# The token search of a mixture-of-experts layer: tile table as weights, lane table moving, sums transposed

## The chip, the cores and the metric

The kernel runs on one core of one Trainium2 chip. The metric is the device time of one execution in microseconds (us). A core has five engines that run side by side and wait for each other by semaphores: TensorE (matrix products; PE in the profile, its weight loads PEld), VectorE (DVE), ScalarE (ACT), GpSimd (POOL) and SyncE (SP, which here starts DMA transfers and reads numbers out of memory). A product on TensorE has two operands in SBUF, the core's working memory of 128 partitions: the *weights* are loaded into the array first (LDWEIGHTS), and then the *moving* operand streams through it, column by column. The sums go to PSUM.

## The reference, cut to what matters

A layer of attention plus a mixture of eight experts over 4096 tokens of 128 numbers. Each token is sent to its two best experts.

```python
scores = x @ gate_w.T                       # x: 4096 tokens x 128, E = 8 experts
mult, idx = _route(scores)                  # the two best experts, with their factors
g = (one_hot(idx, E) * mult[..., None]).sum(axis=1)
h1 = einsum('th,efh->tef', x, w1)
h3 = einsum('th,efh->tef', x, w3)
inter = silu(h1) * h3 * g[:, :, None]
y = einsum('tef,ehf->th', inter, w2)
...
x = x + _L0_attn_ref(xn, ...) + _L0_ffn_ref(xn, ...)
```

## The kernel before

Tokens lie in 32 blocks of 128 (`TT`), one token to a partition, and are handled in two halves `u` (`NU`) of 16 blocks (`UT`). `route(u)` finds each token's two experts and, by counting, the place that the token takes among all tokens of that expert.

The experts' work is cut into 71 tiles of up to 128 tokens (`NSLOT`: 64, and 7 for the remainders). A tile belongs to one expert; within it a token has a *lane*, 0 to 127. So each of the two choices `c` (`TOP`) of a token has an address: a tile (`found_at[u][:, 0]`) and a lane (`found_at[u][:, 1]`).

The *search* turns this around: for every tile and lane it finds the token that belongs there. It does so with products. `in_lanes(u)` builds on VectorE a table `lane[u, c]` of 0 and 1, partition x 128 lanes x 16 blocks (f16, `qb`, `vb`, `oT` and `x2` buffers): 1 where the token has that lane. `slots()` builds a table `tile_{u}_{c}` (called `v`), partition x 71 tiles x 16 blocks: 1 where the token belongs to that tile (L441), multiplied by the token's number (L444). For each block `t` one product of the two sums over the 128 partitions, and 32 products add up in PSUM to `found[:, c]`, lanes by tiles: the number of the one token there, or zero. In all 64 products (2 choices x 2 halves x 16 blocks). In both tables the block is the innermost index, so `[:, :, t]` reads every 16th f16 number, a step of 32 bytes.

`tokens_of(found)` on VectorE makes of it the lists `token` (which row of `table` to gather), `row` (where the result is added) and `first_of`. Ahead of it, while VectorE waits for the products, `slots()` computes `past`, `own_f`, `own` and `fresh` (the expert of each tile, and whether its weights must be fetched anew, L453 to L458).

The order of the instructions is written by hand and is fixed on every engine. Around the search it is:

- on TensorE, 80 products of ones (`busy_late`, L1251) are issued ahead of the search; after it come the first projections of the attention (`pq`, `pqs`, L799), the transposes of `v` (`pvt`, L856), the transposes of gathered tokens (`pxs`, L537) and the experts' first products (L552);
- on VectorE, `tokens_of` is followed by `bias` (L669, L670) and the rotations of `k` and `q` (L813 to L848);
- POOL gathers the tokens of a tile by an indirect DMA (`fetch`, L501), with `token` as its list;
- SP reads `own` and `fresh` and fetches an expert's weights (`weights`, L527); the second and third fetch wait for a gather.

After this comes the long loop over the 71 tiles, in which the experts' products and the attention's work are woven together by a planner; it is not touched.

PSUM is divided into pools: `pa` with five buffers, `ph` with two and `py` with one. `found` lies in `py`, which the `pxs` transposes use afterwards. `busy_late` and later the experts' sums lie in `ph`. In SBUF the tables `tile_{u}_{c}` and `past` use the tag `gT`, with five buffers in turn.

Of the kernel before, what the change touches and what calls it, by code (L numbers as in the profile page):

```python
# [11 lines left out]
F32 = mybir.dt.float32  # L12
# [18 lines left out]
P = 128  # L31
# [16 lines left out]
TOP = 2  # L48
NSLOT = TOP * TT + E - 1
# [35 lines left out]
def attn_moe_kernel(ctx: ExitStack, tc: tile.TileContext, a: dict, out: bass.AP):  # L85
    nc = tc.nc

    const = ctx.enter_context(tc.tile_pool(name="const", bufs=1))
    sb = ctx.enter_context(tc.tile_pool(name="sb", bufs=2))
# [3 lines left out]
    ph = ctx.enter_context(tc.tile_pool(name="ph", bufs=2, space=bass.MemoryType.PSUM))  # L93
    py = ctx.enter_context(tc.tile_pool(name="py", bufs=1, space=bass.MemoryType.PSUM))

    def bc(ap, axis, n):
        shape = list(ap.shape)
        shape.insert(axis, n)
        return ap.unsqueeze(axis).to_broadcast(shape)
# [39 lines left out]
    ident = const.tile([P, P], F32, tag="ident", name="ident")  # L139
# [136 lines left out]
    def tmp(shape, tag, name, dt=F32):  # L276
        return sm.tile([P, *shape], dt, tag=f"r_{tag}", name=f"{tag}_{name}", bufs=NU)
# [114 lines left out]
    lane = {}  # L392
# [10 lines left out]
    def slots():  # L403

        count = tmp([E], "count", 0, I32)
        whole = tmp([E], "whole", 0)  # L410
        nc.vector.tensor_tensor(whole, counts[:, 0], counts[:, 1], ALU.add)
        yield
        nc.vector.tensor_scalar(count, whole, float(P - 1), None, ALU.add)
        yield
        nc.vector.tensor_scalar(count, count, 7, None, ALU.logical_shift_right)
        yield
        nc.vector.tensor_copy(whole, count)
        yield
        end = tmp([E], "end", 0)
        nc.vector.tensor_tensor_scan(end, ones[:, 0:E], whole, 0.0, ALU.mult, ALU.add)  # L420
        yield
        base = tmp([E], "base", 0)
        nc.vector.tensor_tensor(base, end, whole, ALU.subtract)
        yield
        for u in range(NU):
            big = sb.tile([P, TOP, UT, E], F32, tag="rope", name=f"base_{u}", bufs=3)
            nc.vector.tensor_tensor(
                big, hots[:, :, ts(u, UT), :], bc(bc(base, 1, UT), 1, TOP), ALU.mult
            )
            yield  # L430
            at = tmp([TOP, UT], "tile", u)
            nc.vector.tensor_reduce(at, big, AX.X, ALU.add)
            yield
            nc.vector.tensor_tensor(found_at[u][:, 0], found_at[u][:, 0], at, ALU.add)
            yield
        yield True
        found = py.tile([P, TOP, NSLOT], F32, tag="py", name="found")
        for c in range(TOP):
            for u in range(NU):
                v = sb.tile([P, NSLOT, UT], F16, tag="gT", name=f"tile_{u}_{c}", bufs=5)  # L440
                nc.vector.tensor_tensor(  # L441
                    v, ramp[:, 0:NSLOT], bc(found_at[u][:, 0, c], 1, NSLOT), ALU.is_equal
                )
                nc.vector.tensor_tensor(  # L444
                    v, v, bc(number_of[:, ts(u, UT)], 1, NSLOT), ALU.mult
                )
                for t in range(UT):
                    nc.tensor.matmul(  # L448
                        found[:, c], lhsT=lane[u, c][:, :, t], rhs=v[:, :, t],
                        start=(u == 0 and t == 0), stop=(u == NU - 1 and t == UT - 1),  # L450
                    )
        past = sb.tile([P, NSLOT, E], F32, tag="gT", name="past", bufs=5)
        nc.vector.tensor_tensor(past, bc(tile_start, 2, E), bc(end, 1, NSLOT), ALU.is_ge)  # L453
        own_f = tmp([NSLOT], "own_f", 0)
        nc.vector.tensor_reduce(own_f, past, AX.X, ALU.add)
        nc.vector.tensor_scalar(own, own_f, float(E - 1), None, ALU.min)
        nc.vector.tensor_tensor(
            fresh[:, NW_BUF:], own_f[:, NW_BUF:], own_f[:, : NSLOT - NW_BUF], ALU.not_equal  # L458
        )
        tokens_of(found)  # L460

    def tokens_of(found):

        sum_f = tmp([NSLOT], "sum_f", 0)
        nc.vector.tensor_copy(sum_f, found[:, 1])
        nc.vector.tensor_tensor(sum_f, found[:, 0], sum_f, ALU.add)
        nc.vector.scalar_tensor_tensor(token, sum_f, 0.0, sum_f, ALU.is_gt, ALU.subtract)
        nc.vector.tensor_scalar(token, token, NTOK - 1, None, ALU.bitwise_and)
        empty = tmp([NSLOT], "empty", 0)
        nc.vector.scalar_tensor_tensor(empty, sum_f, 0.0, spare, ALU.is_equal, ALU.mult)  # L470
        nc.vector.tensor_tensor(row, token, empty, ALU.add)
        nc.vector.tensor_scalar(first_of, found[:, 0], 0.0, None, ALU.not_equal)
# [710 lines left out]
    with tc.manual_schedule(  # L1183
# [4 lines left out]
        parts = [moments(u) for u in range(NU)]  # L1188
        turns = []
        folds, finding = fold(), slots()  # L1190
        act, dve, pool = nc.scalar, nc.vector, nc.gpsimd
        plan = Plan(
# [200 lines left out]
```

## Time and profile before

| what | us |
|---|---|
| median of three runs | 463.5 |
| the three runs | 462.41, 463.5, 468.3 |
| the profiled execution | 465.26 |
| its span, first to last instruction | 463.5 |
| TensorE, products busy | 419.1 (90%) |
| VectorE busy | 315.4 (68%) |
| ScalarE busy | 254.0 (55%) |
| POOL busy | 241.6 (52%) |

The span is what the profile shows; the execution's own time has 1.8 us more around it. All times "at" something are microseconds from the start of the span. The search's place in it:

| at (us) | what |
|---|---|
| 43.2 to 52.3 | `busy_late` on TensorE |
| 45.1 to 51.7 | the four `lane` tables on VectorE, with other work between |
| 51.7 to 57.5 | the four `tile` tables on VectorE, two instructions each |
| 53.2 to 62.1 | the 64 products of the search |
| 57.4 to 59.3 | `past`, `own_f`, `own`, `fresh` on VectorE |
| 62.1 to 63.7 | `tokens_of` on VectorE |
| 64.5 | the first gather on POOL |
| 69.4 | the first product of the first expert tile |

A line of a timeline reads: start, duration, engine, line and operation, what is written and read, shapes, count, and in brackets how long the engine was idle just before and what ended it. A product's recorded duration is the time from its start to its end, which overlaps the next ones; the time from one start to the next tells how fast they follow. The granted clock is the share of TensorE's full clock that it is given at the time.

### The profile page before, as it was taken

How to read it: one execution, taken by the hardware profiler on the slowest of the kernel's cores; microseconds unless marked ns; L12 is line 12 of the kernel's file. 1: busy time of each engine (PE TensorE's matmuls, PEld its weight loads, DVE VectorE, ACT ScalarE, POOL GpSimd, SP SyncE). 2: the span in 40 equal slices, each digit the busy share in tenths (PEclk: the TensorE clock that was granted, in tenths of full speed). 3: DMA queues.
4: the chain of work that ended last, by engine and by line, in shares of the span. 5: the costliest groups of instructions: out<-in, count | busy, mean ns of one | idle time of the engine just before them, and what ended most of it. 6: DMA issues, size and time to landing. Idle time of an engine off the chain costs nothing.

```text
span 463.5 us, 11704 instructions
## 1 busy us (share of the span) xinstructions
PE 419.1 (90%) x4547; PEld 358.1 (77%) x4547; DVE 315.4 (68%) x750; ACT 254.0 (55%) x716; POOL 241.6 (52%) x210
## 2 busy tenths in 40 slices
PE   9859998999997999999999999999999998999900
PEld 9427966898886899869789888797988897989800
DVE  5698977788788897686676876874868567434300
ACT  1466014888326969534956795339767823553300
POOL 0724237776457454476464466664454657532442
PEclk9986958999999999999999999999999999999975
DMA  8710755226412722352145522451365224516314
GB/s 249 259 47 2 141 125 166 30 25 150 99 19 35 197 39 31 86 144 30 26 96 150 58 26 36 114 127 24 78 148 75 35 37 96 132 18 114 75 17 51
DMA packets 43670, 39.51 MB, mean 85 GB/s; under 512 B 3056, under 2 KB 41968, under 8 KB 43616
## 3 DMA queue, kind: packets, MB, share of 16 engines
q1 hardware_dynamic: 26896, 27.29, 20.7%
q0 software_dynamic: 16720, 11.49, 19.9%
q8 instruction: 36, 0.59, 0.5%
q14 instruction: 18, 0.15, 0.1%
HBM read 60.16 MB, written 11.04 MB: 154 GB/s over the span
## 4 chain that ended last, share of the span: by engine, by line
PE 65%; DVE 13%; ACT 12%; DMA 5%; issue 3%; SPq 0%; POOLq 0%; POOL 0%; DVEq 0%
PE y L578 11%; PE p L552 11%; PE y L552 8%; ACT pr L920 5%; PE pf L1032 5%; PE po L950 5%; DMA out_dram<-sly,row 3%; PE pff L1043 3%; PE ppt L930 3%; PE ps L878 3%; PE found L448 2%; PE px L976 2%; DVE mx L895 2%; PE pgt L265 2%; PE pqs L799 2%
## 5 line engine op out<-in xcount | busy, mean ns | idle before, releaser
L597 POOL DMA_INDIRECT out_dram<-sly,row x71 | 112.3, 1582 | 140.3 <-ACT sly L588 74.6
L501 POOL DMA_INDIRECT slx<-table,token x71 | 71.1, 1001 | 34.8 <-issue 18.5
L562 DVE SCALAR_TENSOR_TENSOR th<-th,p 128x512 f32<-128x512 f32 x71 | 48.6, 684 | 50.2 <-ACT th L561 50.0
L552 PEld LDWEIGHTS p<-slxT,w 128*128 128x128 f32 x568 | 70.2, 192 | 15.4 <-issue 10.2
L578 PEld LDWEIGHTS y<-w,it 128*128 128x128 f32 x568 | 69.6, 191 | 15.7 <-issue 6.4
L578 PE MATMUL y<-w,it 128*128 128x128 f32 x568 | 77.8, 280 | 2.7 <-DVE it L567 2.7
L552 PE MATMUL p<-slxT,w 128*128 128x128 f32 x568 | 78.0, 280 | 1.9 <-issue 1.2
L561 ACT ACTIVATE th<-p 128x512 f32<-128x512 f32 x71 | 44.1, 622 | 57.6 <-PE p L552 49.5
L588 ACT ACTIVATE sly<-y,wt 128x128 f32<-128x128 f32 x71 | 28.0, 394 | 71.5 <-PE y L552 69.3
L567 DVE TENSOR_TENSOR it<-y,th 128x384 f32<-128x384 f32 x70 | 38.8, 554 | 37.9 <-ACT sly L588 37.8
L552 PE MATMUL y<-slxT,w 128*128 128x128 f32 x420 | 58.3, 275 | 0.0
L920 ACT ACTIVATE pr<-ps,mx 128x64 f32<-128x64 f32 (+1 forms) x256 | 54.5, 372 | 0.1
L552 PEld LDWEIGHTS y<-slxT,w 128*128 128x128 f32 x420 | 52.5, 192 | 0.0
L895 DVE TENSOR_REDUCE mx<-ps 128x8 f32<-128x512 f32 x64 | 41.5, 684 | 3.3 <-PE ps L878 2.7
L938 ACT COPY pT<-ppt 128x512 f32<-128x512 f32 (+1 forms) x64 | 35.4, 623 | 0.7
L930 PE MATMUL ppt<-ident,pr 128*128 128x128 f32 x240 | 33.3, 274 | 1.2 <-ACT pr L920 1.1
L1032 PE MATMUL pf<-hT,wf1g 128*128 128x512 f32 x64 | 32.4, 599 | 0.9 <-ACT gT L1036 0.7
L1043 PE MATMUL pff<-pack,gT 128*128 128x128 f32 x256 | 32.7, 275 | 0.0
L961 DVE RECIPROCAL rz<-po 128x256 f32<-128x256 f32 x16 | 28.1, 1756 | 4.2 <-PE po L950 4.0
L1043 PEld LDWEIGHTS pff<-pack,gT 128*128 128x128 f32 x256 | 30.6, 192 | 0.0
L930 PEld LDWEIGHTS ppt<-ident,pr 128*128 128x128 f32 x240 | 27.4, 141 | 3.2 <-ACT pr L920 2.1
L1036 ACT ACTIVATE gT<-pf,bf1g 128x512 f32<-128x512 f32 x32 | 21.8, 693 | 6.8 <-PE pf L1032 6.8
(178 smaller groups left out, 657.2 us busy)
## 6 DMA issues: line engine op xcount, KB each, us to landing
w<-in_wexp_dram SPq DMA_DIRECT2D x71, 704.0 KB
out_dram<-pack SPq DMA_DIRECT2D x1, 2112.0 KB
table<-xn SPq DMA_DIRECT2D x2, 1040.0 KB
x<-in_x_dram SPq DMA_DIRECT2D x8, 256.0 KB
out_dram<-x POOLq DMA_DIRECT2D x8, 256.0 KB
slx<-table,token POOLq DMA_INDIRECT x71, 2.7
out_dram<-sly,row POOLq DMA_INDIRECT x71, 3.3
pack<-in_pack_dram SPq DMA_DIRECT2D x1, 898.0 KB
```

The costliest lines, as they stand in the source:

```text
L501: i = nc.gpsimd.indirect_dma_start(out=self.group[g][:, c, :], out_offset=None, in_=table[:, :], in_offset=bass.IndirectOffsetOnAxis(ap=to ...
L552: nc.tensor.matmul(self.p[j, k][:, c, :], lhsT=self.w[j][:, ts(NFC * k + c, P)], rhs=self.xT[j], start=True, stop=True,)
L561: nc.scalar.activation(th, p, AF.Tanh, scale=0.5)
L562: nc.vector.scalar_tensor_tensor(th, th, 1.0, p, ALU.add, ALU.mult)
L567: nc.vector.tensor_tensor(self.it[j][:, 0:3], self.p.pop((j, 1))[:, 0:3], self.th.pop(j)[:, 0:3], ALU.mult)
L578: nc.tensor.matmul(p[:, 3], lhsT=it[:, c, :], rhs=w[:, 2 * F + c * D : 2 * F + (c + 1) * D], start=(c == 0), stop=(c == NFC - 1),)
L597: nc.gpsimd.indirect_dma_start(out=out[:, :], out_offset=bass.IndirectOffsetOnAxis(ap=row[:, j : j + 1], axis=0), in_=y, in_offset=None, c ...
L895: nc.vector.tensor_reduce(mx, v.rearrange("p s c g k -> p s g c k"), AX.XY, ALU.max, negate=True)
L920: nc.scalar.activation(to[:, s, c0:, g], v[:, s, c0:, g], AF.Exp, bias=mx[:, s, g : g + 1])
L930: nc.tensor.transpose(pp[:, ts(k, P)], v[:, k // 2, k % 2].rearrange("p g k -> p (g k)"), ident)
L1032: nc.tensor.matmul(pf, lhsT=wf1g[:, ts(c, P)], rhs=self.hT[b], start=True, stop=True)
L1043: nc.tensor.matmul(self.pf[b][:, ts(t, D)], lhsT=self.gT[b, c][:, ts(t, P)], rhs=wf2[:, c, :], start=(c == 0), stop=(c == NDF - 1),)
```

## The change

The two tables change places in the products: `tile_{u}_{c}` becomes the weights (71 columns instead of 128) and `lane[u, c]` the moving operand (128 columns instead of 71). The sums then lie with the tiles on the partitions and the lanes along the row, in a PSUM buffer `by_tile` of the pool `ph`. Since `tokens_of` needs lanes on the partitions, the sums are copied by VectorE into an SBUF buffer `lines` (tag `gT`) after `fresh`, and TensorE transposes the two halves of it into `found`, which stays in `py`. What is computed is the same.

```diff
@@ -434,7 +434,7 @@
         yield True
-        found = py.tile([P, TOP, NSLOT], F32, tag="py", name="found")
+        by_tile = ph.tile([NSLOT, TOP, P], F32, tag="ph", name="by_tile")
         for c in range(TOP):
             for u in range(NU):
                 v = sb.tile([P, NSLOT, UT], F16, tag="gT", name=f"tile_{u}_{c}", bufs=5)
...
                 for t in range(UT):
                     nc.tensor.matmul(
-                        found[:, c], lhsT=lane[u, c][:, :, t], rhs=v[:, :, t],
+                        by_tile[:, c], lhsT=v[:, :, t], rhs=lane[u, c][:, :, t],
                         start=(u == 0 and t == 0), stop=(u == NU - 1 and t == UT - 1),
                     )
         past = sb.tile([P, NSLOT, E], F32, tag="gT", name="past", bufs=5)
@@ -457,6 +457,11 @@
         nc.vector.tensor_tensor(
             fresh[:, NW_BUF:], own_f[:, NW_BUF:], own_f[:, : NSLOT - NW_BUF], ALU.not_equal
         )
+        lines = sb.tile([NSLOT, TOP, P], F32, tag="gT", name="lines", bufs=5)
+        nc.vector.tensor_copy(lines, by_tile)
+        found = py.tile([P, TOP, NSLOT], F32, tag="py", name="found")
+        for c in range(TOP):
+            nc.tensor.transpose(found[:, c], lines[:, c], ident[0:NSLOT, 0:NSLOT])
         tokens_of(found)
```

## Prediction

> **What bounds the kernel now.** I read the page first, then the timeline from 52 to 80 us, then the rows of line 448, and last the busy table by window of the clock.
>
> The page says who owns the end:
>
> ```profile
> PE 419.1 (90%) x4547; PEld 358.1 (77%) x4547; DVE 315.4 (68%) x750; ACT 254.0 (55%) x716; POOL 241.6 (52%) x210
> ...
> PE 65%; DVE 13%; ACT 12%; DMA 5%; issue 3%; SPq 0%; POOLq 0%; POOL 0%; DVEq 0%
> PE y L578 11%; PE p L552 11%; PE y L552 8%; ACT pr L920 5%; PE pf L1032 5%; PE po L950 5%; DMA out_dram<-sly,row 3%; PE pff L1043 3%; PE ppt L930 3%; PE ps L878 3%; PE found L448 2%; PE px L976 2%; DVE mx L895 2%; PE pgt L265 2%; PE pqs L799 2%
> ```
>
> TensorE carries 65% of the chain that ends last, and the search (`found`, L448) has 2% of it, some 9 us. Nothing runs beside the search that could fill in: the engines' orders are fixed, and the expert loop cannot start without the list of tokens. The timeline shows the handover:
>
> ```profile
> 55.98 0.74 DVE L441 TENSOR_TENSOR tile<-ramp,at 128x1136 f16<-128x1136 f16 x1
> 56.76 0.75 DVE L444 TENSOR_TENSOR tile<-tile,number_of 128x1136 f16<-128x1136 f16 x1
> ...
> 62.03 0.20 PEld L799 LDWEIGHTS pq<-nT,wallg 128*32 128x32 f32 x8 [0.22 <-issue]
> 62.04 1.08 PE L799 MATMUL pq<-nT,wallg 128*32 128x256 f32 x8
> 62.14 0.23 DVE L465 COPY sum_f<-found 128x71 f32<-128x71 f32 x1 [2.82 <-PE found L448]
> ...
> 63.87 0.20 PEld L799 LDWEIGHTS pqs<-nT,wallg 128*32 128x32 f32 x8 [1.63 <-DVE bias L670]
> ...
> 64.46 1.23 POOL L501 DMA_INDIRECT slx<-table,token  x1 [15.45 <-DVE bias L670]
> ```
>
> VectorE has the last one-hot table at 57.5 us and then idles 2.8 us for TensorE, so the 64 products are what ends last here. Behind them everything queues: VectorE's `sum_f` to `bias`, hence ScalarE's `kb`, POOL's first gather, TensorE's own `pqs`. Whatever the search gains or loses up to 62.14 us moves the rest as a block.
>
> What limits one product? The rows of line 448, the first load alone, and two other lines' rows:
>
> ```profile
> L448 PEld LDWEIGHTS <-lane x64: 142/147/157, 52.1 to 61.7; 128*128 128x128 f16 x64
> L448 PE MATMUL found<-tile,lane x64: 298/317/323, 53.2 to 61.8; 128*128 128x71 f16 x64
> ...
> 52.09 0.15 PEld L448 LDWEIGHTS <-lane 128*128 128x128 f16 x1
> ```
> ```profile
> L683 PEld LDWEIGHTS pbf<-pack,pack x8: 186/192/192, 72.0 to 72.8; 128*128 128x128 f32 x8
> L683 PE MATMUL pbf<-pack,pack x8: 250/250/271, 72.0 to 72.8; 128*128 128x1 f32 x8
> ```
> ```profile
> 54.70:56.00 1.30, 1.30 (x12) 1.00 1.23 178
> 56.00:57.80 1.80, 1.80 (x15) 0.50 1.29 200
> 57.80:61.95 4.15, 4.15 (x32) 0.50 0.94 142
> ```
>
> Starts from 53.2 to 61.8 us over 63 steps: 136 ns for a pair of load and product. The last fence (stretch, then PE busy with its count, then granted clock) shows that the clock falls from 1.00 to 0.50 at 56.0 us and the pace does not change with it. So the array's clock is not the limit; reading an operand is. Which one? The `pbf` rows show a pair that waits for its weights: the product moves one column, eight pairs start within 0.8 us (some 111 ns each), and a load recorded at 192 ns thus holds its path for about 111, 81 less. Line 448's load is recorded at 147, the lone first one too; less the same 81 it holds its path for some 66 ns, half of the 136. Its product is recorded at 317 where `busy_late`'s, of 128 f32 columns, has 275. I conclude that the moving operand sets the pace: 71 columns in 136 ns, 1.92 ns per column. Both tables are read with a step of 16 halves (32 bytes, `[:, :, t]`), which no other row here does. The Trainium skill (Advanced Engine Details and Errata, Memory Cachelines) gives a reason: reads pay when each element lies in a new 16-byte line.
>
> **Part 1: the operands change places.** The moving operand grows from 71 to 128 columns at the same step of 32 bytes. No row shows a moving table of 128 such columns, so I bound it. From below: it streams at the clock, and the pace falls to that or to the load's. From above: loads and products stop overlapping, 381 ns (worked out among the rivals). The row it is nearest to is line 448's own moving read, as step, type and memory are the same: 128 x 1.92 = 245 ns.
>
> Here a rule and the row part. The Trainium skill (TensorE: Matmul & The Clock Gate, Back-to-back issue gap) gives an isolated product N/1.2 ns at half clock: 59 for 71 columns, 107 for 128. By it the new pace would be 107, 64 x (107 - 136) = -1.9 us before the transposes. But the same rule predicts 59 for what the trace shows at 136, so I use the row: 63 x 245 = 15.5 us, plus the last product (0.34 us from its start at 61.80 to VectorE's at 62.14, plus 0.11 for its longer stream), 15.9 in all, against 62.14 - 53.23 = 8.9. That is **+7.0 us**.
>
> The weights shrink from 128 to 71 columns. A rule speaks against this too: the same page (Weight-path perf modes) says that a non-f32 weight of exactly 128 columns is loaded in four chunks of 32 at once; with 71 that ends. Line 448's 66 ns for 128 columns agree with chunks (32 x 1.92 = 61). Loading 71 one after another would be 136 ns by the row's rate, 59 by the page's P/1.2. Either is under 245 and is pulled ahead of the running product, as now: 0. Its cover is the longer stream; without it the price is rival 3. Only the first load loses its head start (it ran at 52.09, before the table; now it waits for the table): +0.1 us.
>
> VectorE's tables come every 1.45 us (0.74 + 0.75 less overlap), while 16 products would take 3.9: tables stay hidden. `past`, `own`, `fresh` end at 59.3 us and SP's first fetch of weights goes at 59.88, unchanged.
>
> **Part 2: copy and transposes.** All of this is new on the chain; nothing covers it, as `by_tile` must be complete first. VectorE's copy of 71 x 256 f32 from PSUM: nearest are `ck` L813 (128x256 f32, PSUM source) at 0.48 and L465 (71 columns) at 0.23; I take 0.45, bounds 0.23 and 0.48. Handing on to TensorE: 0.04 (`tile` to `found` in the chain of waits). Two transposes in the half clock: `pxs` L537 takes 0.51 from its load at 69.12 to ScalarE's 69.64, and the next follows at the pace of `pvt` L856, 1.90 us for eight f32 products, up to 0.24; less some 0.1, as 71 columns move instead of 128. I take 0.65, bounds 0.45 and 0.75. Together **+1.15 us** (0.7 to 1.3). On TensorE `pq` and all after it queue behind the transposes; in the order of instructions of the changed kernel nothing else moves: one copy on VectorE and two transposes come in, while POOL, SP, ScalarE and their DMAs keep their sequence. The shared buffers rotate by one (`ph`, `gT`); their earlier users ended microseconds before, so 0.
>
> **Part 3: the clock.** The granted clock changes in steps of 3.4 us (56.0, 69.65, 73.07, 76.48)[...]. The column rate stays at 0.52 per ns, so the search looks as idle as before and the clock stays at 0.50. Shifting the work by 8 us against these steps changes which products run at half clock between 62 and 77 us: I bound this at -1.5 to +1.5 us (one window of half-speed work either way) and take 0.
>
> **The sum.** 7.0 + 0.1 + 1.15 = 8.25 us. The profiled execution took 465.26 us (span 463.5, 1.8 around it) and becomes 473.5. It lies 1.8 above the median of the runs, 463.5, so the same addition to the median gives 471.8, +1.8%. Catching up later would need a transfer that is late now; the only ones between 60 and 78 us are SP's fetches, of which the second and third wait for the gathers and so move with the block.
>
> **The rivals.**
> 1. The pace does not rise. If the 128-column weight load were the limit, or if both reads shared one path (199 columns either way), 64 pairs would take 107 to 136 ns each. For it: the load has the same 32-byte step, and the load and product start together. Against it: the lone load takes as long as those beside products (0.15 us), so they don't share a path, and 66 ns of it leave no limit at 136. It gives -1.9 to 0, plus 1.25: 462.9 to 464.8 us.
> 2. The search stays as I say, but the clock recovers earlier or later: 470.3 to 473.3. It is in my range.
> 3. The other side of the 2% line: the narrower load, no longer in chunks, cannot hide, because it is read with the same step and the two reads alternate. Then a pair costs 245 + 136 = 381 ns, 64 x 245 = +15.7, plus 1.25: 480 us. It decides from a pace of 261 ns on: 2% of 463.5 is 9.3, less 1.25 is 8.0, over 64 is 125 ns more than 136. Against it: loads run beside products on every other line.
> That the change does not do what it says is excluded by the order of instructions, which shows 64 loads of `tile` with products 71x128.
>
> **How the numbers follow.** Forecast (pace 235 to 250, clock within its bounds) 0.77; rival 1, 0.16; rival 3 or something like it, 0.05; anything else 0.02. About 2%, 9.3 us, is what a measurement of this kernel can tell from no change. Of the forecast's 0.77 a quarter lies above 472.8 (late clock, a dearer copy): 0.19, with rival 3 and half the rest 0.25 slower. Faster by over 2% has no mechanism: 0.01. Within 2%: 0.74. The forecast alone spans 469.5 to 474.5; to leave out no more than 2 in 10 the range takes in the upper part of rival 1: 464.5 to 475.
>
> **What would show it.** Right: `by_tile` products starting every 240 to 250 ns from 53.3 to about 69 us; loads of `tile` recorded at over 200 ns (136 + 81) and hidden; VectorE idle for some 9.8 us before the copy; `sum_f` at about 70.4 us. A pace of 107 to 136 shows rival 1; over 261, rival 3. A shift at `sum_f` that is over 2 us away from the shift at the end would show that the block does not move rigidly, and the forecast would be wrong after the search, not in it.

## The result, and the profile after

| | before | after |
|---|---|---|
| median of 20 runs (us) | 465.53 | 472.05 |
| lowest and highest | 462.41, 468.84 | 469.36, 472.59 |
| profiled execution | 465.26 | 472.32 |
| its span | 463.5 | 470.5 |

The changed kernel is slower: the ratio to the kernel before is 1.0115, with a 95% interval of 1.0094 to 1.0137, so some 5.4 us. The medians alone differ by 6.5, the two profiled executions by 7.1: the runs of each kernel lie in two groups (before 462.4 to 466.3 and 467.7 to 468.8, after 469.4 to 470.6 and 471.5 to 472.6), so these two differences depend on which group a run fell into, and the ratio is the better measure.

The page after, busy times and chain:

```profile
PE 425.1 (90%) x4549; PEld 362.7 (77%) x4549; DVE 315.6 (67%) x751; ACT 254.4 (54%) x716; POOL 241.7 (51%) x210
...
PE 66%; DVE 12%; ACT 11%; DMA 7%; issue 3%; SPq 0%; POOLq 0%; POOL 0%; DVEq 0%
PE p L557 11%; PE y L583 11%; PE y L557 8%; PE pf L1037 5%; PE po L955 5%; DMA out_dram<-sly,row 5%; ACT pr L925 5%; PE ppt L935 3%; PE by_tile L448 3%; PE pff L1048 3%; PE ps L883 3%; PE px L981 2%; PE pgt L265 2%; PE pqs L804 2%; DVE mx L900 2%
```

The search is now 3% of the chain. TensorE is 6 us busier, VectorE hardly: two product instructions and one copy more, nothing else. The timeline of the handover:

```profile
52.66 14.78 PEld L448 LDWEIGHTS <-tile 128*71 128x71 f16 x64 [0.95 <-DVE tile L444]
52.66 15.21 PE L448 MATMUL by_tile<-lane,tile 128*71 128x128 f16 x64 [0.76 <-DVE tile L444]
...
67.91 0.42 DVE L461 COPY lines<-by_tile 71x256 f32<-71x256 f32 x1 [9.16 <-PE by_tile L448]
...
68.39 0.50 PE L464 MATMUL found<-ident,lines 71*128 71x71 f32 x2 [0.51 <-DVE lines L461]
...
68.93 0.23 DVE L470 COPY sum_f<-found 128x71 f32<-128x71 f32 x1 [0.59 <-PE found L464]
...
70.22 1.24 POOL L506 DMA_INDIRECT slx<-table,token  x1 [21.51 <-DVE empty L475]
```

VectorE waits 9.16 us for the products in place of 2.82. From the first product to `sum_f` it was 62.14 - 53.23 = 8.91 us and is 68.93 - 52.66 = 16.27: **+7.36**. Of this the products have (67.91 - 52.66) - 8.91 = 15.25 - 8.91 = 6.34 and copy with transposes 68.93 - 67.91 = 1.02. The rows of line 448 (duration as minimum, median, maximum, then the first and last start):

```profile
L448 PEld LDWEIGHTS <-tile x64: 208/209/230, 52.7 to 67.2; 128*71 128x71 f16 x64
L448 PE MATMUL by_tile<-lane,tile x64: 411/413/500, 52.7 to 67.5; 128*71 128x128 f16 x64
```

The starts lie 233 ns apart (from the second at 52.98 to the last at 67.47 us, 14.5 us over 62 steps; the first step is 0.32 us), where they were 136 before. The load of 71 columns is recorded longer than that of 128 was (209 for 147).

After `sum_f` the shift between the two profiles does not stay the same:

| instruction | before | after | shift (us) |
|---|---|---|---|
| first product of the search | 53.23 | 52.66 | -0.57 |
| `sum_f` | 62.14 | 68.93 | +6.79 |
| first copy of `slxT` | 68.81 | 75.59 | +6.78 |
| first `it` from `y_-1` | 74.46 | 80.13 | +5.67 |
| first `mx` | 76.28 | 81.10 | +4.82 |
| end of the span | 463.5 | 470.5 | +7.0 |

Two microseconds are given back and lost again. The windows of the granted clock show it (stretch, its length, PE busy with its count, clock, DMA share, GB/s), first before, then after:

```profile
66.24:69.65 3.41, 3.06 (x16) 0.50 0.28 65
69.65:73.06 3.41, 3.30 (x26) 1.00 0.89 277
73.06:76.48 3.42, 3.42 (x27) 0.50 0.70 241
76.48:79.89 3.41, 3.02 (x26) 1.00 0.19 39
```
```profile
75.89:79.30 3.41, 3.39 (x27) 1.00 0.92 307
79.30:82.72 3.42, 3.42 (x42) 1.00 0.70 225
82.72:86.13 3.41, 1.87 (x13) 1.00 0.07 20
86.13:89.54 3.41, 3.29 (x22) 0.50 0.32 44
```

Before, `y_-1` and the first scores fall into a window at half clock; after, the same work runs at full clock (79.30 to 82.72), but a later window is at half. The six products of `y_-1` take 1.51 us before and 0.91 after, the 16 of `ps` behind them 1.50 and 0.82.

### The profile page after: what moved, and what is told of

It is laid out like the page before. It is cut to its first block, busy times and chain, and to the rows that moved or that the text cites. A ratio compares the mean times of both kernels' runs of the same rounds, so it can differ in the third digit from the quotient of the medians.

```text
span 470.5 us, 11710 instructions
## 1 busy us (share of the span) xinstructions
PE 425.1 (90%) x4549; PEld 362.7 (77%) x4549; DVE 315.6 (67%) x751; ACT 254.4 (54%) x716; POOL 241.7 (51%) x210
## 4 chain that ended last, share of the span: by engine, by line
PE 66%; DVE 12%; ACT 11%; DMA 7%; issue 3%; SPq 0%; POOLq 0%; POOL 0%; DVEq 0%
PE p L557 11%; PE y L583 11%; PE y L557 8%; PE pf L1037 5%; PE po L955 5%; DMA out_dram<-sly,row 5%; ACT pr L925 5%; PE ppt L935 3%; PE by_tile L448 3%; PE pff L1048 3%; PE ps L883 3%; PE px L981 2%; PE pgt L265 2%; PE pqs L804 2%; DVE mx L900 2%
```

## The experiments

My theory was the prediction's: a moving operand that is read with a step of 32 bytes sets the pace of a product. Rival W: the load of the weights sets it. Rival N: columns cost as such, whatever the step.

**Four kernels, each with one of the tables stored block by block.** The step goes from one operand at a time, in both arrangements; the instructions keep their count and shapes. For the lanes in the changed kernel:

```diff
-            lane[u, c] = v = sb.tile([P, P, UT], F16, tag=tag, ...)
-            nc.vector.tensor_tensor(v, ramp, ...)
+            lane[u, c] = v = sb.tile([P, UT, P], F16, tag=tag, ...)
+            nc.vector.tensor_tensor(v.rearrange("p t l -> p l t"), ramp, ...)
...
-                        by_tile[:, c], lhsT=v[:, :, t], rhs=lane[u, c][:, :, t],
+                        by_tile[:, c], lhsT=v[:, :, t], rhs=lane[u, c][:, t, :],
```

The others do the same for the tile table or in the arrangement of before.

> The changed kernel with the lane table stored block by block, so that the moving operand is read without a step; the weights keep their step of 32 bytes. The table is written with a step instead, by the same instruction (estimate from half its rate: 2.1 us in place of 1.22, four times, +3.7 us before the search). Theory (the step of the moving read sets the pace): from 233 ns a pair to 128-136 ns, where the narrow load of weights takes over (recorded at 209 ns, 81 of it latency). Rival W (the load of 71 weights sets the pace): stays 233. Rival N (the number of moving columns costs as such, whatever the step): stays 233.

> The changed kernel with the tile table stored block by block: the weights are read without a step, the moving lanes keep theirs. The tile tables take longer on VectorE (estimate 1.2 us for 0.75), which the search hides but for the first, +1 us. Theory: the pace stays at 233 ns, the weight load is recorded at about 140 ns (59 + 81) in place of 209. Rival W: the pace falls with the load, by some 70 ns or more. Rival N: stays 233.

> The kernel before with the lane table stored block by block: weights of 128 columns without a step, moving tiles with their step of 32 bytes. Theory: the pace stays at 136 ns; the load is recorded at about 100 ns, as the bf16 load of L870 is, in place of 147. Rival W: the pace falls below 110 ns. Rival N: stays 136. In time the four lane tables cost about 3.7 us more.

> The kernel before with the tile table stored block by block: moving 71 columns without a step, weights of 128 columns with theirs. Theory: within a burst of 16 products the pace falls from 136 to 60-75 ns (a load of 66, or 71 columns at half clock, 59); the search is then limited by VectorE, whose tables take about 1.2 us an instruction: its end moves by less than 2 us either way. Rival W: the pace stays at 136. Rival N: stays at 136.

Measured, with the weight load's recorded median and the median time from one product's start to the next (for the kernel before the mean is 136). Each packed kernel ran once:

| kernel | step of moving, of weights (bytes) | load (ns) | pace (ns) | single run (us) |
|---|---|---|---|---|
| before | 32, 32 | 147 | 137 | 465.34 beside it |
| before, lanes packed | 32, 2 | 127 | 130 | 497.19 |
| before, tiles packed | 2, 32 | 165 | 62 | 497.0 |
| after | 32, 32 | 209 | 233 | |
| after, tiles packed | 32, 2 | 159 | 232 | 500.68 |
| after, lanes packed | 2, 32 | 231 | 133 | 497.09 |

The rows of the last two, line 449 and line 448:

```profile
L449 PEld LDWEIGHTS <-tile x64: 133/159/167, 62.0 to 95.6; 128*71 128x71 f16 x64
L449 PE MATMUL by_tile<-lane,tile x64: 411/412/426, 62.0 to 95.8; 128*71 128x128 f16 x64
```
```profile
L448 PEld LDWEIGHTS <-tile x64: 209/231/232, 84.4 to 92.8; 128*71 128x71 f16 x64
L448 PE MATMUL by_tile<-lane,tile x64: 291/337/393, 84.4 to 92.8; 128*71 128x128 f16 x64
```

Taking the step from the weights leaves the pace (137 to 130, 233 to 232); taking it from the moving operand about halves it (137 to 62, 233 to 133). W and N fall. The recorded loads without a step, 159 and 127 ns, are longer than the 140 and 100 that I expected; the pace does not depend on them.

What sets the two paces that remain is shown for one. The 133 ns are the same at a granted clock of 0.50 (42 starts) and of 1.00 (21), so it is not the array's own stream; the load of the 71 columns is left. A load of 128 columns with the same step fits into 62 ns. This agrees with the rule of the Trainium skill (TensorE: Matmul & The Clock Gate, Weight-path perf modes) that only weights of 128 columns are loaded the fast way. The 62 itself may be this load or the stream: all these products ran at a clock of 0.50, where 71 columns would take an estimated 107 x 71 / 128 = 59 ns (107 is measured with `both in twos` below). In the changed kernel the slower, narrow load stays hidden, as the moving read's 233 is longer still.

The totals say nothing of the products: all four took 32 to 35 us more than the kernel before beside them, and the tables on VectorE account for it (four lane tables: 4 x (9.37 - 1.22) = 32.6), far from my estimates of 1.2 to 2.1 us an instruction. The lane tables' row in `after, lanes packed` (before: 1218 ns):

```profile
L401 DVE TENSOR_TENSOR lane<-ramp,at x4: 9252/9373/9502, 44.9 to 73.5; 128x2048 f16<-128x2048 f16 x4
```

**Two kernels that only delay.** Does a shift of the search move the end by as much? Both add 54 products of the same tables to the kernel before, into a spare PSUM buffer: one after the search (shown), the other ahead of its last 16 products.

```diff
+        again = ph.tile([P, NSLOT], F32, tag="ph", name="again")
+        for t in range(54):
+            nc.tensor.matmul(
+                again, lhsT=lane[u, c][:, :, t % UT], rhs=v[:, :, t % UT],
+                start=(t == 0), stop=(t == 53),
+            )
```

> The kernel before, with 54 further products of the same two tables after the 64, into a spare PSUM buffer that nobody reads: at 136 ns each they delay what follows on TensorE by 7.3 us, about what the change did between the first product and sum_f (7.4 us), without changing an operand. But VectorE's sum_f waits for found alone, so only TensorE's later work is held up, not tokens_of; pq and pqs come 7.3 us later, and pvt, pxs and the expert loop behind them. Theory (the block after the search moves rigidly, and the granted clock takes back or adds up to 1.5 us): slower than before by 1.2 to 1.6% of the time, as the change is. Rival (something later absorbs part of any delay, a transfer or a wait that was late anyway): under 1%.

> The kernel before with 54 further products of the same tables ahead of the last 16 of the search, into a spare PSUM buffer that nobody reads: found, and with it tokens_of, comes 7.3 us later, as much as the change did, with no operand changed. Theory (the shift moves all that follows, and the granted clock, which moves in steps of 3.4 us, gives about 2 us of it back): +0.9 to +1.4% of the time, as the change. Rival (a rigid shift): +1.6%. Rival (the exchange itself helps or hurts later work): under 0.7% or over 1.7%.

After the search: 1.0116 (1.0086 to 1.0147), a little below my 1.2 to 1.6%. Ahead of its end: 1.0143 (1.0096 to 1.0189), a little above my 0.9 to 1.4%. In the second the trace shows `found` late as wanted:

```profile
59.55 7.54 PE L450 MATMUL again<-tile,lane 128*128 128x71 f16 x54
66.91 2.38 PE L456 MATMUL found<-tile,lane 128*128 128x71 f16 x16
```

`sum_f` is at 69.32, +7.2 from 62.14, and the end moves by about what the change's does: the intervals overlap. So the exchange has no effect on the total that can be told from its delay. The interval reaches the rigid 1.6%, so the totals do not decide whether 2 us are given back. The trace shows them given back at the same place, with no operand exchanged: the shift is +7.18 at `sum_f` and +5.22 at the first `mx`, where the changed kernel has +6.79 and +4.82. The first kernel is a warning against reading causes out of totals: there `sum_f` was not held up, the first two `cq` (the rotations of `q`) were not late, the third came 3.5 us late (71.73 for 68.27), the first `slxT` 4.4 us, and yet the end moved as much.

**A shorter search by small instructions.** If the moving read is the limit, the tile table should lie without a step and be written without one.

```diff
-                v = sb.tile([P, NSLOT, UT], F16, tag="gT", ...)
-                nc.vector.tensor_tensor(v, ramp[:, 0:NSLOT], ..., ALU.is_equal)
-                nc.vector.tensor_tensor(v, v, ..., ALU.mult)
+                v = sb.tile([P, UT, NSLOT], F16, tag="gT", ...)
                 for t in range(UT):
+                    k = u * UT + t
+                    nc.vector.tensor_scalar(
+                        v[:, t, :], tiles, tile_of[u][:, c, t : t + 1], numbers[:, k : k + 1],
+                        ALU.is_equal, ALU.mult,
+                    )
...
-                        found[:, c], lhsT=lane[u, c][:, :, t], rhs=v[:, :, t],
+                        found[:, c], lhsT=lane[u, c][:, :, t], rhs=v[:, t, :],
```

> The operands stand as in the kernel before, but the tile table is stored block by block and written without a step: for each block one VectorE instruction compares 71 numbers with the token's tile and multiplies by the token's number (64 instructions of 71 columns in place of 8 of 1136). Theory: the product's pace falls to about 62 ns as with the packed tiles, TensorE follows VectorE block by block, and the search ends some 0.4 us after the last table. With 0.08 to 0.13 us for one VectorE instruction the tables take 5.1 to 8.3 us in place of 5.8, so sum_f comes 1.5 to 4.5 us earlier than before and the time falls by 0.3 to 1.0%. Rival (the small instructions cost 0.2 us each, as lone ones of this size are recorded): the tables take 12.8 us, sum_f comes 2.5 us later, +0.5%.

1.0123 (1.0091 to 1.0156). The rival's price for one instruction was the right one, its total was not (it had `sum_f` 2.5 us later and +0.5%):

```profile
51.27 13.42 DVE L445 TENSOR_SCALAR tile<-tiles,tile,pack 128x71 f16<-128x71 f16 x64
```

One instruction takes 0.21 us, the tables 13.4 in place of 5.8, and `sum_f` comes at 66.42, 4.3 us later.

**Tables in groups.** The blocks of a table can lie in groups of 4 (or 2) side by side: the step falls to 8 (or 4) bytes, and VectorE still writes unit steps.

```diff
-                v = sb.tile([P, NSLOT, UT], F16, tag="gT", ...)
+                v = sb.tile([P, UT // 4, NSLOT, 4], F16, tag="gT", ...)
...
-                        found[:, c], lhsT=lane[u, c][:, :, t], rhs=v[:, :, t],
+                        found[:, c], lhsT=lane[u, c][:, :, t], rhs=v[:, t // 4, :, t % 4],
```

> The operands stand as in the kernel before. In the tile table four blocks lie side by side, so that the moving operand is read with a step of 8 bytes in place of 32; the two VectorE instructions keep their count, size and innermost unit step. Theory (a moving read is slow where each element lies in a new 16-byte line, as the Trainium skill's Memory Cachelines says): two columns share a line, the pace falls to 60-70 ns, the search ends about 1.4 us after the last table, behind fresh; sum_f comes 2 to 3 us earlier than before if VectorE keeps its 0.75 us, and the time falls by 0.4 to 0.7%. Rival (any step costs): the pace stays above 100 ns and the time within 0.3%. Second rival (VectorE loses half its rate at runs of four, 1.2 us an instruction): the tables take 4 us longer, +0.2 to +0.6%.

> As the kernel with the tile table in fours, and the lane table and the ramp that both are compared with in fours too; POOL's ramp shrinks from 2048 to 512 columns. Theory: the pace is that of the tile table in fours, the load of weights falls from 147 to about 100 ns; the time is that of tiles in fours, within 0.2%. Rival (loads of 66 ns still set the pace there): the pace falls by 5 ns or more.

> The changed kernel with both tables in fours: 71 weights and 128 moving columns, both with a step of 8 bytes. Theory (the step, not the exchange, made the change dear): the pace falls from 233 to 107-115 ns at half clock, where the array's own rate takes over (128 columns at half clock), and below 80 at full clock; the search ends about 2 us after the last table; copy and transposes stay at 1.0 us. Rival (any step costs): the pace stays above 150.

> The changed kernel with both tables in fours, timed. In its one look the search kept the granted clock at 1.00 until 63.4 us [...]. Theory (the operands' order with 128 moving columns holds the clock through the search, and this is worth more than the 1 us of copy and transposes): faster than before by 0.3 to 1.0% in nearly all runs, and faster than the kernel with only the tables in fours and the operands of before, which was 0.9% slower. Rival (one lucky look): 0.5 to 1.2% slower, like the other kernels with a short search.

> The changed kernel with both tables in pairs: the moving operand has a step of 4 bytes, four columns to a 16-byte line. From the paces with 32 bytes (1.70 ns a column besides 15) and 8 bytes (0.79 besides 16) a line costs 1.6 to 1.7 ns, so a column 0.42 and a product 16 + 54 = 70 ns at full clock, 107 at half. The search then waits for VectorE's tables and ends 1.3 us earlier than in fours[...]. Theory: faster than in fours by 0.1 to 0.4%, the best of all. Rival (VectorE is slower at runs of two): its instructions over 0.8 us, no gain over fours.

| kernel | moving columns, step | pace (ns) | `sum_f` (us) | ratio to before |
|---|---|---|---|---|
| before, tiles in fours | 71, 8 bytes | 72 | 58.94 | 1.0097 (1.0066 to 1.0127) |
| before, both in fours | 71, 8 | 69 | 58.17 | 1.0087 (1.0056 to 1.0118) |
| after, both in fours | 128, 8 | 117 | 61.54, 61.52 | 0.9997 (0.9966 to 1.0027) |
| after, both in twos | 128, 4 | 107 at half clock, 57 at full | 59.41 | 1.0118 (1.0078 to 1.0159) |

VectorE kept its 0.75 us throughout, and the pace behaved as the step asks, in both arrangements. With 8 bytes and the exchanged operands:

```profile
L453 PEld LDWEIGHTS <-tile x64: 141/143/167, 53.0 to 60.2; 128*71 128x71 f16 x64
L453 PE MATMUL by_tile<-lane,tile x64: 293/296/318, 53.0 to 60.4; 128*71 128x128 f16 x64
```

So the exchange is dear only with the wide step. But every expectation of a faster kernel fell: a search that ends 3 to 4 us earlier gives a time that is 1% longer, and the first, single run of `after, both in fours` with 462.65 us was a lucky one (the fourteen later ones took 463.47 to 471.49). Nor did its clock stay up: the later profile has 0.50 from 54.32 to 57.74 us, in the middle of the search. The profile of `both in fours` (469.83 us, an ordinary run of its ten) shows where the gain goes; first the timeline, then the windows of the clock (the last two are later ones):

```profile
58.17 0.22 DVE L470 COPY sum_f<-found 128x71 f32<-128x71 f32 x1
...
62.22 1.26 POOL L506 DMA_INDIRECT slx<-table,token  x1 [14.29 <-DVE sq L820]
...
65.17 0.33 PE L542 MATMUL pxs<-ident,slx 128*128 128x128 f32 x1 [1.48 <-DMA slx<-table,token]
```
```profile
62.65:66.06 3.41, 1.37 (x13) 1.00 0.30 77
66.06:69.47 3.41, 2.62 (x11) 0.50 0.47 120
69.47:72.89 3.42, 3.42 (x17) 0.50 0.97 316
72.89:76.30 3.41, 3.41 (x28) 0.50 0.49 149
76.30:79.71 3.41, 3.11 (x28) 1.00 0.07 20
...
83.12:86.54 3.42, 3.42 (x25) 0.50 0.23 24
147.98:151.39 3.41, 3.29 (x23) 0.50 0.31 38
```

The list `token` is ready at 59.15 us, the first gather starts at 62.22 all the same. Besides the list it reads `table`, whose two writes were issued at 48.4 and 48.9 us. On POOL's queue an instruction stands ahead of the gather that waits for the two semaphores which these writes raise. It comes through at 61.3 us here, 2.2 us after the list, and at 63.5 in the kernel before, where the list was ready at 63.14:

```profile
L506 POOLq EVENT_SEMAPHORE  x1: 43/43/43, 61.3 to 61.3; - x1
```
```profile
L501 POOLq EVENT_SEMAPHORE  x1: 43/43/43, 63.5 to 63.5; - x1
```

In both profiles, and in those of the other kernels with tables in groups, the gather starts 0.86 or 0.87 us after the end of this wait. So it waits for the write of `table`, and an earlier list does not help it.

TensorE then stands idle for the gathered tokens (1.48 us, and 1.35 before the next), its window from 62.65 is 40% busy, and the clock is at 0.50 for the next 10 us. The shift against before goes from -3.98 us at `sum_f` over -2.24 at the first gather to +1.31 at the first `mx`. Two more windows at half clock, at 83.12 and 147.98 us, take it to +2.92 and +4.46, and the end has +4.4. The profile of `after, both in twos` shows the same sequence: list at 60.41, gather at 64.03, a window that is 18% busy, a clock of 0.50 from 66.95 to 80.60, +2.78 at the first `mx`. That the idle time brings the clock down is argued from this order alone; in the kernel before a window that was busy for 3.30 of 3.41 us (69.65 to 73.06) is followed by one at half clock too. The profile of `tiles in fours` happens to be the fastest of its ten runs (462.27; the others 467.3 to 470.9), and there the clock was back at 65.97 and stayed until 141.06. What happened in its nine others is not shown; the same cause is likely.

## Why the prediction was right, by its steps

- **What bounds the kernel.** That the 64 products end last held: VectorE's wait for them grew by 6.34 us, as much as the products. That all else queues behind them held for `sum_f` and `slxT`, not for the first gather (below).
- **The moving read sets the pace.** Shown, by the four packed kernels. That the narrow load is not chunked and still hides held too: recorded at 209, 128 after the 81 of latency, where I had 136; alone it sets a pace of 133. For the wide load I had 66; it fits into 62.
- **Its size was a little off.** I scaled the whole 136 ns with the columns, to 245, and named 240 to 250 as the sign of being right. The two paces give (233 - 137) / 57 = 1.68 ns a column and 17 besides that do not grow. Part 1 is thus 6.34 (with the first load) in place of 7.1. The first load's lost head start is seen as 500 ns for the first product in place of 413.
- **Copy and transposes.** 1.02 in place of 1.15: the copy 0.42 (0.45), the transposes from 68.39 to 68.93 0.54 (0.65).
- **The clock.** Taken as 0, bounded at 1.5 us either way. The two profiles differ by -2.0 us at the first `mx`, a little outside that bound, and by nothing at the end. The ratio's 5.4 us against 7.36 in the search suggests that some 2 us are given back on average. That the clock does this is the only cause seen in the traces; how often it does is not shown.
- **Rigid motion.** I said that no transfer between 60 and 78 us is late enough to give time back. TensorE's side held: the shift is the same at `sum_f` and at the first `slxT`. But I overlooked a transfer: the write of `table` was still under way, and before, the first gather waited for it until 63.5 us and started 1.3 us after its list. After the change it starts 0.3 after the list, so it moved by 5.8 us and not by 6.8. It cost nothing in this direction; it is what swallows a shorter search.
- **The sum.** 8.25 was 0.9 too high in the search and took nothing for the clock; it compares with 5.4 us by the ratio. That 471.8 lies next to the measured median of 472.05 is luck: I added to 463.5, the median of three runs, where twenty runs have 465.53, and a base that was 2.0 too low made up for a sum that was too high. The range, from 464.5, also took in almost no change at all. So it is the pace that speaks for the mechanism, not the total.

Rival 1 needed the load or a shared path as the limit; both fall with the packed kernels. Rival 3 needed loads and products to alternate; then a load that is recorded 50 ns shorter (159 for 209) would have shortened the pair, and it left 232 of 233.

## What to carry to other kernels

Which operand of a product is read with a step matters more than which is wider: compare the time from start to start with the columns, find out which operand's step it follows, and group the innermost index until the pace follows the clock (here a step of 4 bytes). A table that a step has to be taken out of should be regrouped, not transposed in the write: groups kept VectorE's 0.75 us, the transposed write took 5 and more. And a gain ahead of the main loop is only a gain if what follows is ready for it: here the first gather waited for another transfer, and with a clock at half a search that ended 4 us earlier became an end 4 us later.

## What the runs showed that I had not expected

- A moving f16 operand costs some 1.7 ns a column at a step of 32 bytes, at either granted clock, and (117 - 72) / 57 = 0.79 at 8 bytes; at 4 bytes the pace follows the clock (57 ns for 128 columns at 1.00, 107 at 0.50). The Trainium skill (Advanced Engine Details and Errata, Memory Cachelines) lets two accesses to a line suffice; at 8 bytes they do not quite, and the numbers look like some 1.6 ns for each line of 16 bytes.
- VectorE writing f16 with a step of 256 bytes takes 9.37 us for 128x2048, 7.7 times the 1.22 with a unit step; with 142 bytes 5.37 for 128x1136 in place of 0.74. No estimate of half the rate comes near that.
- One window of 3.4 us at a granted clock of 0.50 inside the loop costs 1.5 to 1.7 us. The shift against before jumps by that much wherever a profile has such a window and before has none: 4.83 to 6.38 us in the changed kernel (at 86.13), 5.23 to 6.89 in the kernel with the longer search (at 150.94), -4.50 to -2.90 with tiles in fours (at 141.06), 2.92 to 4.46 with both in fours (at 147.98). Kernels whose totals differ by less than this may differ in nothing but where these windows fall.
- Three kernels with a shorter search were slower than before (ratios 1.0087 to 1.0118), in the profiles of two of them after a late gather, an idle TensorE and a clock that stays at 0.50 for three or four windows of 3.4 us. The kernel's time is not a monotone function of the search's end: a shorter search can make it longer.
